# Loading tile 0 of the expert layers without the plan, and adding layer 1's residual behind the product

## The chip, the core and the metric

The kernel runs on one core of one Trainium2 chip. The metric is the device time of one execution in microseconds (us). The programs use five instruction streams: TensorE (PE in the profile, with its weight loads as PEld), VectorE (DVE), ScalarE (ACT), GpSimd (POOL) and SyncE (SP), which here only issues DMAs and reads values into registers. Everything is computed in float32.

## The reference

The input x is 4 batches of 512 tokens of width 256. Four blocks are added to it in turn: an attention with an MLP, a first mixture of experts, a second attention, a second mixture of experts. The change touches the two mixtures. Cut to what they compute:

```python
# layer 0: h = layernorm(x) @ W_in + b_in; 8 experts, two chosen per token
topv, topi = jax.lax.top_k(softmax(t @ W_gate + b_gate), 2)      # topv normalized to sum 1
mid  = relu(einsum('nd,edh->neh', t, W1) + b1)                   # 256 -> 1024
eout = einsum('neh,ehd->ned', mid, W2) + b2                      # 1024 -> 256
out  = einsum('ne,ned->nd', route, eout) @ W_out + b_out
...
# layer 1: 8 experts, one chosen per token
scores, idx = max(gates, axis=1), argmax(gates, axis=1)
h = gelu(x @ W1[idx] + b1[idx])                                  # 256 -> 512
o = (h @ W2[idx] + b2[idx]) * scores                             # 512 -> 256
x = x + o
```

## The kernel before

**Sorting tokens by expert.** Each token is computed only by the experts that it chose. `Dispatch.send` (L299) works out, for a group of tokens, the place of each in a DRAM buffer `sent`, in which expert e owns the rows from e * 2048 on. It counts the earlier tokens of each expert in `seen` by two small matmuls (`rank`, L311 and L312), adds the start of the expert's region (L317), picks the chosen expert's place (L318 to L321), casts it to an integer `slot` (L322), and scatters the rows by indirect DMAs from GpSimd (L325). A row has 258 numbers: the 256 features, the token's share for that expert, and the index of the row that the result goes back to. Before that, `sent` was filled with rows that lead nowhere (`clear`).

**The plan.** `Dispatch.plan` (L339) makes a list of tiles of 256 rows from the counts: a matmul `pn` (L343), its copy `n` (L345), a comparison of n with `full` (L347: how many tiles each expert has), a running sum, and for each tile its expert and its first row (L357 to L373). The number of tiles and these two lists are read into registers (`values_load` L369, `value_load` L379 and L380).

**The tiles.** `Dispatch.tiles` (L375) runs 20 tiles in layer 0 and 11 in layer 1 (`run`, L448), and up to 23 and 15 under a condition on the count. `load(i)` (L378) issues the DMAs of a tile, all on SP's queue: `rows` from `sent` (L382, 258 KB), the expert's W1 and W2 (`load_w1` L116, `load_w2` L121; together 2 MB in layer 0, 1 MB in layer 1) and its biases b1 and b2 (L387, L388; b2 is spread over all 128 partitions, 128 KB). In layer 1 it also gathers the residual of each row, which lies in `kept` in DRAM, into `y` by two indirect DMAs from GpSimd (L396). `turn` (L410) transposes the rows on TensorE (L414) and copies them to `inT` on VectorE (L416). `hidden` (L465) multiplies by W1 (L472) and applies bias and function into `mid`: on ScalarE (L476), in layer 0 on VectorE (L474) for every second chunk. It has three PSUM buffers `pm`. `give` (L419) prepares y: share * b2 on ScalarE in layer 0 (L429), share * b2 + residual on VectorE in layer 1 (L427). `project` (L479) multiplies mid by W2 (L485), and `take` (L431) adds share * product to y on VectorE (L432) and scatters y by an indirect DMA from GpSimd (L435): in layer 0 to `came`, in layer 1 to the output.

**Order and buffers.** The loop of `run` is: hidden(i), load(i + 1), turn(i + 1), give(i). Weights, biases, inT and mid have two buffers each, rows has two in layer 0 and four in layer 1, y two in layer 0 and four in layer 1. The weights' pool `wpool` also holds, by the same two tags, keys and values of the first stage, and between the layers what comes back from `came` (`bring`, L884, whose loads go by L888). Where no order is written out by hand, a scheduler places each engine's instructions by estimated times; an engine, and SP's queue, then runs them strictly in that order. The first stage is written out by hand for all engines except SP, the attention of layer 1 (from L1058 on) for TensorE only. So where SP's loads land in its queue is the scheduler's choice, except for those marked `keep_in_program_order`.

Of the kernel before, what the change touches and what calls it, by code (L numbers as in the profile page):

```python
# [25 lines left out]
NE = 8  # L26
# [17 lines left out]
def xattn_ffn_kernel(ctx: ExitStack, tc: tile.TileContext, a: dict, out: bass.AP):  # L44
# [69 lines left out]
    def load_w1(ap, n):  # L114
        w = wpool.tile([P, NC, n], F32, tag="w1", name="w1")
        nc.sync.dma_start(w, ap.rearrange("(c p) n -> p c n", p=P))  # L116
        return w
# [48 lines left out]
    def constants():  # L166
        nc.gpsimd.memset(nowhere[:, 0:TO], 0.0)
        nc.gpsimd.iota(
            nowhere[:, TO:ROW].bitcast(I32), pattern=[[0, 1]], base=NOWHERE, channel_multiplier=0
        )  # L170
        nc.gpsimd.memset(before, 1.0)
        nc.gpsimd.affine_select(
            before, before, pattern=[[1, P]], compare_op=ALU.is_gt, fill=0.0, base=0, channel_multiplier=-1
        )
        nc.gpsimd.memset(ones, 1.0)
        for e in range(NE):
            nc.gpsimd.memset(falling[:, :, e : e + 1], float(NE - e))
            nc.gpsimd.memset(region[:, :, e : e + 1], float(e * CAP))
        for j in range(CAP // TT):
            nc.gpsimd.memset(full[:, :, j : j + 1], float(j * TT))  # L180
        for i in range(TILES0):
            nc.gpsimd.memset(number[:, i, :], float(i))

# [96 lines left out]
    class Dispatch:  # L280
# [18 lines left out]
        def send(self, b, tts, chosen, psum, tag):  # L299

            pool, seen = self.pool, self.seen
            n, picks = chosen.shape[1:3]
            these = slice(tts[0], tts[-1] + 1)
            both = chosen[:, :, 0, :]
            if picks == 2:
                both = small.tile([P, n, NE], F32, tag="both", name="both")
                nc.vector.tensor_tensor(both, chosen[:, :, 0, :], chosen[:, :, 1, :], ALU.add)
            for t in tts:
                nc.vector.tensor_tensor(seen[:, t + 1, :], seen[:, t, :], both[:, t - tts[0], :], ALU.add)
            rank = psum.tile([P, n, NE], F32, tag=tag, name="rank")  # L310
            nc.tensor.matmul(rank, before, both, start=True, stop=False)  # L311
            nc.tensor.matmul(rank, ones, seen[:, these, :], start=False, stop=True)  # L312
            place = small.tile([P, n, NE], F32, tag="place", name="place")
            mine = small.tile([P, n, picks, NE], F32, tag="mine", name="mine")
            at = small.tile([P, n, picks], F32, tag="at", name="at")
            slot = pool.tile([P, n, picks], I32, tag="slot", name="slot", bufs=2)
            nc.vector.tensor_tensor(place, rank, region[:, 0:n, :], ALU.add)  # L317
            nc.vector.tensor_tensor(  # L318
                mine, chosen, place.unsqueeze(2).to_broadcast([P, n, picks, NE]), ALU.mult
            )  # L320
            nc.vector.tensor_reduce(at, mine, AX.X, ALU.add)  # L321
            nc.vector.tensor_copy(slot, at)  # L322
            for t in tts:
                for k, r in enumerate(self.rows):
                    i = nc.gpsimd.indirect_dma_start(  # L325
                        out=sent[self.layer][:, :],
                        out_offset=bass.IndirectOffsetOnAxis(ap=slot[:, t - tts[0], k : k + 1], axis=0),
                        in_=r[:, t, :],
                        in_offset=None,
                    )  # L330

                    tc.declare_no_dep(i.ins, group=self.group, reason="rows of their own")
                    tc.add_to_no_dep_group(self.group, i.ins)
            if tts[-1] == NT - 1:
                nxt = pool.tile([P, NT + 1, NE], F32, tag=f"seen{(b + 1) % 2}", name=f"seen{b + 1}")
                nc.vector.tensor_copy(nxt[:, 0, :], seen[:, NT, :])
                self.seen = nxt

        def plan(self, psum, tag):  # L339

# [1 line left out]
            pn = psum.tile([P, NE], F32, tag=tag, name="pn")  # L342
            nc.tensor.matmul(pn, ones, self.seen[:, 0, :], start=True, stop=True)  # L343
            n = small.tile([P, NE], F32, tag="n", name="n")
            nc.vector.tensor_copy(n, pn)  # L345
            more = small.tile([P, NE, CAP // TT], F32, tag="more", name="more")
            nc.vector.tensor_tensor(more, over(n, CAP // TT), full, ALU.is_gt)  # L347
            count = small.tile([P, NE], F32, tag="count", name="count")
# [23 lines left out]
            nc.vector.tensor_copy(self.row, first)  # L372
            nc.vector.tensor_copy(self.expert, e)  # L373

        def tiles(self, n_tiles, usual, n, w1_all, w2_all, b1_all, b2_all, func, tp, midp, pm_pool, po_pool, also):  # L375


            def load(i):  # L378
                e = nc.sync.value_load(self.expert[0:1, i : i + 1], min_val=0, max_val=NE - 1)  # L379
                row = nc.sync.value_load(self.row[0:1, i : i + 1], min_val=0, max_val=NE * CAP)  # L380
                rows = tp.tile([P, TT // P, ROW], F32, tag="rows", name="rows", bufs=2 + 2 * self.layer)
                nc.sync.dma_start(rows, sent[self.layer][bass.ds(row, TT), :].rearrange("(s p) w -> p s w", p=P))  # L382
                b1 = tp.tile([P, n // P], F32, tag="b1", name="b1")
                b2 = tp.tile([P, D], F32, tag="b2", name="b2")

                def biases():
                    nc.sync.dma_start(b1, b1_all[:, bass.ds(e * (n // P), n // P)])  # L387
                    nc.sync.dma_start(b2, b2_all[bass.ds(e, 1), :].to_broadcast([P, D]))  # L388

                y = None  # L390
                if self.layer == 1:
                    biases()
                    y = tp.tile([P, TT // P, D], F32, tag="y", name="y", bufs=4)
                    for u in range(TT // P):

                        nc.gpsimd.indirect_dma_start(  # L396
                            out=y[:, u, :],
                            out_offset=None,
                            in_=kept[:, :],
                            in_offset=bass.IndirectOffsetOnAxis(ap=rows[:, u, TO:ROW].bitcast(I32), axis=0),  # L400
                            bounds_check=N - 1,
                            oob_is_err=False,
                        )
                w1 = load_w1(w1_all[bass.ds(e, 1)].rearrange("o d n -> (o d) n"), n)
                w2 = load_w2(w2_all[bass.ds(e, 1)].rearrange("o k d -> (o k) d"), n)
                if self.layer == 0:
                    biases()
                return rows, w1, w2, b1, (b2, y)

            def turn(rows):  # L410
                ps = psT.tile([P, NC, TT // P, P], F32, tag="psT", name="psIn")
# [5 lines left out]
                return inT  # L417

            def give(rows, w2, added, mid):  # L419
                b2, y = added  # L420
                here = y is not None
                if not here:
                    y = tp.tile([P, TT // P, D], F32, tag="y", name="y")
                for u in range(TT // P):
                    share = rows[:, u, D:TO]
                    if here:
                        nc.vector.scalar_tensor_tensor(y[:, u, :], b2, share, y[:, u, :], ALU.mult, ALU.add)  # L427
                    else:
                        nc.scalar.mul(y[:, u, :], b2, share)  # L429

                def take(u, po):  # L431
                    nc.vector.scalar_tensor_tensor(  # L432
                        y[:, u, :], po, rows[:, u, D:TO], y[:, u, :], ALU.mult, ALU.add
                    )
                    i = nc.gpsimd.indirect_dma_start(  # L435
                        out=came[self.layer][:, :],
                        out_offset=bass.IndirectOffsetOnAxis(ap=rows[:, u, TO:ROW].bitcast(I32), axis=0),
                        in_=y[:, u, :],
                        in_offset=None,
                        bounds_check=came[self.layer].shape[0] - 1,  # L440
                        oob_is_err=False,
                    )
                    tc.declare_no_dep(i.ins, group=f"take{self.layer}", reason="rows of their own")
                    tc.add_to_no_dep_group(f"take{self.layer}", i.ins)

                project(mid, w2, po_pool, take)
# [66 lines left out]
    with tc.tile_pool(name="l0a", bufs=2) as lp, tc.tile_pool(name="l0tmp", bufs=2) as tp, tc.tile_pool(  # L513
# [274 lines left out]
        for b in range(B):  # L788
# [11 lines left out]
                *(memory[2:3] if b == 2 else ()), *((gates[3], chain(pad(8), memory[3])) if b == 3 else ()),  # L800
            )

    layer0.close()


# [40 lines left out]
    with tc.tile_pool(name="f0tmp", bufs=2) as tp, tc.tile_pool(  # L846
# [4 lines left out]
        send.plan(po_pool, "po")  # L851
        early = chain(places(heads), fetch(0))
        send.tiles(
            TILES0, 2 * N // TT + 4, HD, a["L0_ffn_W1"], a["L0_ffn_W2"], a["b1_0_col"], a["L0_ffn_b2"], AF.Relu,
            tp, midp, pm_pool, po_pool, early,
        )

# [6 lines left out]
    with tc.tile_pool(name="l1a", bufs=2) as lp, tc.tile_pool(name="l1s", bufs=1) as sp, tc.tile_pool(  # L864
# [193 lines left out]
        with tc.manual_schedule(engines={mybir.EngineType.PE}):  # L1058
# [12 lines left out]
            for i in range(-AHEAD, groups + 1):  # L1071
                if i + AHEAD in (NG, 2 * NG):
                    side.append(prepares[(i + AHEAD) // NG + 1])
                for n in range(2 * NT):
# [18 lines left out]
                            side += [finish(i // NG - 1), choose(i // NG - 1)]  # L1093
                    else:
                        step()
            while side:
                step()


    with tc.tile_pool(name="f1tmp", bufs=2) as tp, tc.tile_pool(  # L1100
# [3 lines left out]
    ) as pm_pool, tc.tile_pool(name="f1p_o", bufs=3, space=bass.MemoryType.PSUM) as po_pool:  # L1104
        send.plan(psT, "psT")
        send.tiles(
            TILES1, N // TT + 3, H1, a["L1_ffn_W1"], a["L1_ffn_W2"], a["b1_1_col"], a["L1_ffn_b2"], AF.Gelu,
            tp, midp, pm_pool, po_pool, iter(()),
        )

# [55 lines left out]
```

## Time and profile before

| | |
|---|---|
| runs of before (3) | 1078.2, 1081.53, 1085.03 us; median 1081.53 |
| the profiled execution | 1082.0 us |
| its span in the profile | 1080.3 us |
| PE busy | 981.3 us, 91% of the span |
| DVE, ACT, POOL busy | 519.2, 360.6, 295.5 us |
| layer 0's tiles, first product to last | 316.65 to 603.87 us |
| layer 1's tiles, first product to last | 978.22 to 1073.2 us |
| rows<-sent, landing | 2.8 us (median of 31) |
| weights, layer 0 / layer 1, landing | 7.1 / 6.1 us (medians of 40 and 22) |
| b2, landing | 6.7 us (median of 31) |
| gather of the residual / scatter to the output, landing | 5.2 / 4.1 us (medians of 22 and 22) |

The profile is of one execution. The page gives busy times of each engine, the chain of work that ended last and the costliest groups of instructions by source line. A line of the timeline has the start in us, the duration, the engine, the source line, the operation with output and inputs, the shape, the number of instructions run together, and in brackets the idle time of the engine before it and what ended it. "SPq" lines are SP issuing a DMA; the data lands later, and landing times run from the issue. "issue" means that nothing which the profile shows was waited for.

### The profile page before, as it was taken

Reading aid. Unit: us, or ns where it says so; the run is one execution under the profiler, and the core shown is the slowest. Engines: PE = TensorE matmul, PEld = TensorE weight load, DVE = VectorE, ACT = ScalarE, POOL = GpSimd, SP = SyncE. Lnnn points to the kernel's source line nnn. Section 1 sums busy time; section 2 is a strip of 40 time slices with the busy share of each in tenths; the row PEclk is TensorE's granted clock in tenths of the full one; section 3 lists DMA queues with packets and bytes.
Section 4 is the critical chain, followed back from the end, with each engine's and each line's share of the span. In section 5 each row is a group of like instructions: output and inputs, shape, how many; then the busy total and the mean of one; then the engine's idle time right before and its main releaser. Section 6 shows DMA issues by size and latency. Waiting matters only on the chain.

```text
span 1080.3 us, 14074 instructions
## 1 busy us (share of the span) xinstructions
PE 981.3 (91%) x4843; PEld 653.4 (60%) x4843; DVE 519.2 (48%) x1329; ACT 360.6 (33%) x628; POOL 295.5 (27%) x333
## 2 busy tenths in 40 slices
PE   5889999999759999999999689999999999948986
PEld 3556667575548888888888544333434334336775
DVE  5775675554642222222222168667767767132222
ACT  4444242324211111222211023555555565602221
POOL 3330242333332222111111273003623102113443
PEclk9989999999979999999999889999999999867999
DMA  6679999931164566656555402001101000017773
GB/s 203 222 183 249 247 248 242 247 104 39 40 211 145 192 204 202 202 188 206 180 187 187 165 21 58 11 6 56 39 12 58 20 2 20 20 48 228 218 202 94
DMA packets 113708, 146.00 MB, mean 135 GB/s; under 512 B 15060, under 2 KB 95197, under 8 KB 113632
## 3 DMA queue, kind: packets, MB, share of 16 engines
q1 hardware_dynamic: 107296, 130.29, 42.5%
q0 software_dynamic: 6336, 14.75, 4.1%
q8 instruction: 41, 0.67, 0.3%
q14 instruction: 35, 0.29, 0.1%
HBM read 86.71 MB, written 58.80 MB: 135 GB/s over the span
## 4 chain that ended last, share of the span: by engine, by line
PE 48%; issue 25%; POOL 9%; DMA 8%; DVE 7%; SPq 1%; ACT 1%; POOLq 0%; DVEq 0%
PE sc L958 12%; PE av L978 6%; PE pm L598 5%; PE po L604 4%; POOL came L435 3%; PE scT L958 3%; PE pm_sid L556 2%; PE pf L564 2%; DMA came<-y,rows 1%; PE pq L919 1%; PE psTr L877 1%; PE pd L579 1%; DMA rows<-sent 1%; DMA sent<-rows,slot 1%; PE po L1011 1%
## 5 line engine op out<-in xcount | busy, mean ns | idle before, releaser
L472 PE MATMUL pm<-inT,w 128*128 128x256 f32 x816 | 188.7, 390 | 14.2 <-DVE inT L416 8.3
L965 DVE TENSOR_REDUCE nm<-sc 128x1 f32<-128x512 f32 x256 | 164.2, 683 | 62.4 <-PE scT L958 60.0
L472 PEld LDWEIGHTS pm<-inT,w 128*128 128x128 f32 x816 | 158.4, 195 | 40.4 <-DVE inT L416 11.3
L485 PE MATMUL po<-w,mid 128*128 128x256 f32 x816 | 181.3, 379 | 0.0
L962 ACT ACTIVATE ex<-scT 128x512 f32<-128x512 f32 x256 | 138.6, 597 | 100.0 <-PE scT L958 99.2
L485 PEld LDWEIGHTS po<-w,mid 128*128 128x128 f32 x816 | 152.8, 190 | 19.6
L958 PE MATMUL sc<-kT,qT 32*128 32x512 f32 x512 | 161.6, 636 | 0.1
L958 PE MATMUL scT<-qT,kT 32*128 32x512 f32 x512 | 161.7, 649 | 0.0
L476 ACT ACTIVATE mid<-pm,b 128x256 f32<-128x256 f32 x124 | 58.7, 474 | 179.8 <-PE pm L472 146.8
L435 POOL DMA_INDIRECT came<-y,rows x40 | 39.3, 982 | 240.2 <-DVE y L432 240.2
L958 PEld LDWEIGHTS sc<-kT,qT 32*128 32x128 f32 x512 | 52.7, 183 | 61.2 <-DVE nm L965 46.5
L432 DVE SCALAR_TENSOR_TENSOR y<-po,rows,y 128x256 f32<-128x256 f32 x62 | 29.7, 481 | 123.8 <-PE po L485 120.8
L474 DVE TENSOR_SCALAR mid<-pm,b 128x256 f32<-128x256 f32 x80 | 38.7, 483 | 102.4 <-PE pm L472 102.4
L240 POOL TENSOR_TENSOR rstd<-var,halved 128x4 f32<-128x4 f32 (+1 forms) x32 | 27.9, 876 | 211.0 <-DVE var L239 188.9
L325 POOL DMA_INDIRECT sent<-rows,slot x48 | 48.0, 1000 | 90.4 <-DVE slot L322 43.0
L978 PE MATMUL av<-ex,va 128*32 128x512 f32 x512 | 70.7, 618 | 0.0
L598 PE MATMUL pm<-hT,w 128*128 128x512 f32 x128 | 63.8, 627 | 2.4 <-DVE hT L511 2.4
L604 PE MATMUL po<-w,mid 128*128 128x256 f32 x256 | 60.8, 383 | 0.0
L429 ACT ACTIVATE y<-b,rows 128x256 f32<-128x256 f32 x40 | 18.1, 500 | 127.5 <-DMA b<-in_L_ffn_b 108.1
L958 PEld LDWEIGHTS scT<-qT,kT 32*128 32x128 f32 x512 | 52.5, 186 | 12.8 <-issue 11.2
L604 PEld LDWEIGHTS po<-w,mid 128*128 128x128 f32 x256 | 48.1, 192 | 10.3 <-issue 4.5
L978 PEld LDWEIGHTS av<-ex,va 128*32 128x32 f32 x512 | 10.6, 109 | 50.6 <-issue 40.4
(236 smaller groups left out, 1182.5 us busy)
## 6 DMA issues: line engine op xcount, KB each, us to landing
w<-in_L_ffn_W SPq DMA_DIRECT2D x40, 1024.0 KB, 7.1
sent<-nowhere SPq DMA_DIRECT2D x32, 1161.0 KB, 19.8
w<-in_L_ffn_W SPq DMA_DIRECT2D x22, 512.0 KB, 6.1
rows<-sent SPq DMA_DIRECT2D x31, 258.0 KB, 2.8
y<-came SPq DMA_DIRECT2D x8, 512.0 KB, 7.9
b<-in_L_ffn_b SPq DMA_DIRECT2D x31, 128.0 KB, 6.7
x<-in_x SPq DMA_DIRECT2D x4, 512.0 KB, 5.4
c<-in_ctx SPq DMA_DIRECT2D x4, 512.0 KB, 7.1
```

What stands on the lines that cost most here:

```text
L325: i = nc.gpsimd.indirect_dma_start(out=sent[self.layer][:, :], out_offset=bass.IndirectOffsetOnAxis(ap=slot[:, t - tts[0], k : k + 1], axi ...
L435: i = nc.gpsimd.indirect_dma_start(out=came[self.layer][:, :], out_offset=bass.IndirectOffsetOnAxis(ap=rows[:, u, TO:ROW].bitcast(I32), ax ...
L472: nc.tensor.matmul(pm, w1[:, c, ts(k, P)], inT[:, c, :], start=c == 0, stop=c == NC - 1)
L474: nc.vector.tensor_scalar(mid[:, k, :], pm, bias[:, k : k + 1], 0.0, ALU.add, ALU.max)
L476: nc.scalar.activation(mid[:, k, :], pm, func, bias=bias[:, k : k + 1])
L485: nc.tensor.matmul(po, mid[:, k, ts(t, P)], w2[:, k, :], start=k == 0, stop=k == n - 1)
L598: nc.tensor.matmul(pm, w1_mlp[:, c, ts(k, P)], hT[:, c, :], start=c == 0, stop=c == NC - 1)
L604: nc.tensor.matmul(po, mid[:, k, ts(t, P)], w2_mlp[:, k, :], start=k == 0, stop=k == HD // P - 1)
L958: nc.tensor.matmul(sc, stay, move, start=True, stop=True)
L962: nc.scalar.activation(ex, sc, AF.Exp, scale=1.0 / DH**0.5)
L965: nc.vector.tensor_reduce(nm[:, t, head, 0:1], sc, AX.X, ALU.max, negate=True)
L978: nc.tensor.matmul(av[32 * head : 32 * head + 32, :], vas[b % 2][:, t, 4 * g + head, :], exs.pop((t, head)), start=t == 0, stop=t == NT - 1,)
```

## The change

- Tile 0 of a layer is now always of expert 0 and begins at row 0: `full` gets -1 for expert 0's first tile, so that this tile exists even with no token. Its addresses are constants.
- `ahead` issues tile 0's W1 and W2. It is called at the end of the first stage for layer 0, and in front of the last steps of the attention for layer 1. Tile 0's biases are issued before its rows.
- In `send`, the counts for the next batch are copied before the rank matmuls instead of behind the scatters; in `plan`, the copy of the counts is kept in program order.
- In layer 1 the residual is gathered into buffers `x` of its own (three), y has three buffers instead of four and is prepared by ScalarE in both layers, and `take` adds the residual on VectorE after the product.

The diff:

```diff
--- before.py
+++ after.py
@@ -178,6 +178,8 @@
             nc.gpsimd.memset(region[:, :, e : e + 1], float(e * CAP))
         for j in range(CAP // TT):
             nc.gpsimd.memset(full[:, :, j : j + 1], float(j * TT))
+
+        nc.gpsimd.memset(full[:, 0, 0:1], -1.0)
         for i in range(TILES0):
             nc.gpsimd.memset(number[:, i, :], float(i))
 
@@ -307,6 +309,10 @@
                 nc.vector.tensor_tensor(both, chosen[:, :, 0, :], chosen[:, :, 1, :], ALU.add)
             for t in tts:
                 nc.vector.tensor_tensor(seen[:, t + 1, :], seen[:, t, :], both[:, t - tts[0], :], ALU.add)
+            if tts[-1] == NT - 1:
+                nxt = pool.tile([P, NT + 1, NE], F32, tag=f"seen{(b + 1) % 2}", name=f"seen{b + 1}")
+                nc.vector.tensor_copy(nxt[:, 0, :], seen[:, NT, :])
+                self.seen = nxt
             rank = psum.tile([P, n, NE], F32, tag=tag, name="rank")
             nc.tensor.matmul(rank, before, both, start=True, stop=False)
             nc.tensor.matmul(rank, ones, seen[:, these, :], start=False, stop=True)
@@ -331,10 +337,6 @@
 
                     tc.declare_no_dep(i.ins, group=self.group, reason="rows of their own")
                     tc.add_to_no_dep_group(self.group, i.ins)
-            if tts[-1] == NT - 1:
-                nxt = pool.tile([P, NT + 1, NE], F32, tag=f"seen{(b + 1) % 2}", name=f"seen{b + 1}")
-                nc.vector.tensor_copy(nxt[:, 0, :], seen[:, NT, :])
-                self.seen = nxt
 
         def plan(self, psum, tag):
 
@@ -342,7 +344,8 @@
             pn = psum.tile([P, NE], F32, tag=tag, name="pn")
             nc.tensor.matmul(pn, ones, self.seen[:, 0, :], start=True, stop=True)
             n = small.tile([P, NE], F32, tag="n", name="n")
-            nc.vector.tensor_copy(n, pn)
+
+            tc.keep_in_program_order(nc.vector.tensor_copy(n, pn))
             more = small.tile([P, NE, CAP // TT], F32, tag="more", name="more")
             nc.vector.tensor_tensor(more, over(n, CAP // TT), full, ALU.is_gt)
             count = small.tile([P, NE], F32, tag="count", name="count")
@@ -372,40 +375,60 @@
             nc.vector.tensor_copy(self.row, first)
             nc.vector.tensor_copy(self.expert, e)
 
-        def tiles(self, n_tiles, usual, n, w1_all, w2_all, b1_all, b2_all, func, tp, midp, pm_pool, po_pool, also):
-
+        def ahead(self, n, w1_all, w2_all):
+
+
+            def weights(its):
+                return (
+                    load_w1(w1_all[its].rearrange("o d n -> (o d) n"), n),
+                    load_w2(w2_all[its].rearrange("o k d -> (o k) d"), n),
+                )
+
+            self.first, self.weights = weights(slice(0, 1)), weights
+
+        def tiles(self, n_tiles, usual, n, b1_all, b2_all, func, tp, midp, pm_pool, po_pool, also):
+
+            weights = self.weights
 
             def load(i):
-                e = nc.sync.value_load(self.expert[0:1, i : i + 1], min_val=0, max_val=NE - 1)
-                row = nc.sync.value_load(self.row[0:1, i : i + 1], min_val=0, max_val=NE * CAP)
-                rows = tp.tile([P, TT // P, ROW], F32, tag="rows", name="rows", bufs=2 + 2 * self.layer)
-                nc.sync.dma_start(rows, sent[self.layer][bass.ds(row, TT), :].rearrange("(s p) w -> p s w", p=P))
+                if i:
+                    e = nc.sync.value_load(self.expert[0:1, i : i + 1], min_val=0, max_val=NE - 1)
+                    row = nc.sync.value_load(self.row[0:1, i : i + 1], min_val=0, max_val=NE * CAP)
+                    its, at, to, b1s = bass.ds(e, 1), bass.ds(e, 1), bass.ds(row, TT), bass.ds(e * (n // P), n // P)
+                else:
+                    its, at, to, b1s = slice(0, 1), slice(0, 1), slice(0, TT), slice(0, n // P)
+                direct = self.layer == 1
+                rows = tp.tile([P, TT // P, ROW], F32, tag="rows", name="rows", bufs=4 if direct else 2)
                 b1 = tp.tile([P, n // P], F32, tag="b1", name="b1")
                 b2 = tp.tile([P, D], F32, tag="b2", name="b2")
+                w = []
 
                 def biases():
-                    nc.sync.dma_start(b1, b1_all[:, bass.ds(e * (n // P), n // P)])
-                    nc.sync.dma_start(b2, b2_all[bass.ds(e, 1), :].to_broadcast([P, D]))
-
-                y = None
-                if self.layer == 1:
+                    nc.sync.dma_start(b1, b1_all[:, b1s])
+                    nc.sync.dma_start(b2, b2_all[at, :].to_broadcast([P, D]))
+
+                if not i:
                     biases()
-                    y = tp.tile([P, TT // P, D], F32, tag="y", name="y", bufs=4)
+                nc.sync.dma_start(rows, sent[self.layer][to, :].rearrange("(s p) w -> p s w", p=P))
+                if direct and i:
+                    biases()
+                w = self.first if not i else weights(its)
+                if not direct and i:
+                    biases()
+                x = None
+                if direct:
+                    x = tp.tile([P, TT // P, D], F32, tag="x", name="xr", bufs=3)
                     for u in range(TT // P):
 
                         nc.gpsimd.indirect_dma_start(
-                            out=y[:, u, :],
+                            out=x[:, u, :],
                             out_offset=None,
                             in_=kept[:, :],
                             in_offset=bass.IndirectOffsetOnAxis(ap=rows[:, u, TO:ROW].bitcast(I32), axis=0),
                             bounds_check=N - 1,
                             oob_is_err=False,
                         )
-                w1 = load_w1(w1_all[bass.ds(e, 1)].rearrange("o d n -> (o d) n"), n)
-                w2 = load_w2(w2_all[bass.ds(e, 1)].rearrange("o k d -> (o k) d"), n)
-                if self.layer == 0:
-                    biases()
-                return rows, w1, w2, b1, (b2, y)
+                return rows, *w, b1, (b2, x)
 
             def turn(rows):
                 ps = psT.tile([P, NC, TT // P, P], F32, tag="psT", name="psIn")
@@ -417,21 +440,17 @@
                 return inT
 
             def give(rows, w2, added, mid):
-                b2, y = added
-                here = y is not None
-                if not here:
-                    y = tp.tile([P, TT // P, D], F32, tag="y", name="y")
+                b2, x = added
+                y = tp.tile([P, TT // P, D], F32, tag="y", name="y", bufs=2 if x is None else 3)
                 for u in range(TT // P):
-                    share = rows[:, u, D:TO]
-                    if here:
-                        nc.vector.scalar_tensor_tensor(y[:, u, :], b2, share, y[:, u, :], ALU.mult, ALU.add)
-                    else:
-                        nc.scalar.mul(y[:, u, :], b2, share)
+                    nc.scalar.mul(y[:, u, :], b2, rows[:, u, D:TO])
 
                 def take(u, po):
                     nc.vector.scalar_tensor_tensor(
                         y[:, u, :], po, rows[:, u, D:TO], y[:, u, :], ALU.mult, ALU.add
                     )
+                    if x is not None:
+                        nc.vector.tensor_tensor(y[:, u, :], y[:, u, :], x[:, u, :], ALU.add)
                     i = nc.gpsimd.indirect_dma_start(
                         out=came[self.layer][:, :],
                         out_offset=bass.IndirectOffsetOnAxis(ap=rows[:, u, TO:ROW].bitcast(I32), axis=0),
@@ -800,6 +819,8 @@
                 *(memory[2:3] if b == 2 else ()), *((gates[3], chain(pad(8), memory[3])) if b == 3 else ()),
             )
 
+        send.ahead(HD, a["L0_ffn_W1"], a["L0_ffn_W2"])
+
     layer0.close()
 
 
@@ -851,7 +872,7 @@
         send.plan(po_pool, "po")
         early = chain(places(heads), fetch(0))
         send.tiles(
-            TILES0, 2 * N // TT + 4, HD, a["L0_ffn_W1"], a["L0_ffn_W2"], a["b1_0_col"], a["L0_ffn_b2"], AF.Relu,
+            TILES0, 2 * N // TT + 4, HD, a["b1_0_col"], a["L0_ffn_b2"], AF.Relu,
             tp, midp, pm_pool, po_pool, early,
         )
 
@@ -1093,6 +1114,7 @@
                             side += [finish(i // NG - 1), choose(i // NG - 1)]
                     else:
                         step()
+            send.ahead(H1, a["L1_ffn_W1"], a["L1_ffn_W2"])
             while side:
                 step()
 
@@ -1104,7 +1126,7 @@
     ) as pm_pool, tc.tile_pool(name="f1p_o", bufs=3, space=bass.MemoryType.PSUM) as po_pool:
         send.plan(psT, "psT")
         send.tiles(
-            TILES1, N // TT + 3, H1, a["L1_ffn_W1"], a["L1_ffn_W2"], a["b1_1_col"], a["L1_ffn_b2"], AF.Gelu,
+            TILES1, N // TT + 3, H1, a["b1_1_col"], a["L1_ffn_b2"], AF.Gelu,
             tp, midp, pm_pool, po_pool, iter(()),
         )
```

## The prediction

> **What bounds the kernel now.** I read the page first: matmuls are busy for 91% of the span, so time can come only from stretches where TensorE waits. Near the change these are the start of each layer's expert tiles and the eleven tiles of layer 1. The waits from 960 us to the end (who, for what: total us, times, longest):
>
> ```profile
> DVE y L427 <- DMA y<-kept,rows: 55.8, 12, 8.0
> PE pm L472 <- DVE inT L416: 8.3, 7, 2.6
> ```
>
> VectorE stands at L427 until the gathered residual has landed. The windows of layer 1, cut at tile starts (stretch, length, then busy us of PE, PEld, DVE, ACT, POOL; granted clock, DMA share, GB/s):
>
> ```profile
> 1004.90:1012.35 7.45, 7.45 (x36) 6.36 (x37) 2.33 (x6) 1.90 (x4) 3.71 (x4) 1.00 0.73 217
> 1028.60:1038.80 10.20, 7.60 (x36) 6.38 (x36) 2.25 (x6) 1.90 (x4) 4.08 (x5) 0.97 0.73 195
> 1056.90:1066.00 9.10, 7.59 (x37) 6.36 (x37) 2.24 (x6) 1.90 (x4) 4.06 (x5) 1.00 0.55 164
> ```
>
> A tile holds about 7.4 us of TensorE and takes up to 10.2. The timeline of one shows why: the copy that TensorE needs for the next tile is queued behind L427.
>
> ```profile
> 1054.93 0.88 DVE L427 SCALAR_TENSOR_TENSOR y<-b,rows,y 128x256 f32<-128x256 f32 x2 [7.05 <-DMA out_x<-y,rows]
> ...
> 1056.12 0.68 DVE L416 COPY inT<-psIn 128x512 f32<-128x512 f32 x1
> ...
> 1056.86 3.72 PE L472 MATMUL pm<-inT,w 128*128 128x256 f32 x16 [1.70 <-DVE inT L416]
> ```
>
> The two starts, layer 0 and layer 1 (rows issued, weights issued, first product):
>
> ```profile
> 310.83 0.41 SPq L382 DMA_DIRECT2D rows<-sent  x1
> 311.51 0.38 SPq L116 DMA_DIRECT2D w<-in_L_ffn_W  x1
> 316.65 9.51 PE L472 MATMUL pm<-inT,w 128*128 128x256 f32 x32 [1.85 <-DMA w<-in_L_ffn_W]
> ```
>
> ```profile
> 967.54 0.96 POOL L325 DMA_INDIRECT sent<-rows,slot  x1 [0.30 <-issue]
> 970.22 0.41 SPq L382 DMA_DIRECT2D rows<-sent  x1
> 978.22 5.46 PE L472 MATMUL pm<-inT,w 128*128 128x256 f32 x12 [4.12 <-DMA w<-in_L_ffn_W]
> 980.33 1.28 ACT L476 ACT_TABLE_LOAD   x1 [20.63 <-PE pm L472]
> ```
>
> Both rows loads wait for the last scatter to land (967.54 to 970.22: 2.7 us), not for the plan; the weights, issued behind them, land last. Finally the landing of b2, asked of line 388 in layer 1, on which the forecast turns:
>
> ```profile
> DMA to landing us min/median/max: 3.7/5.2/5.6
> ```
>
> **What the Trainium skill says.** "DMA: Bandwidth & Descriptors", section "Issuing engines are not separate DMA queues": DMAs from every engine run on the same 16 DMA engines and interleave, so b2 waits behind weights, rows and gathers. The 3.7 against 5.6 us agrees. "ScalarE: Activation LUTs", "What ACT_TABLE_LOAD costs": about 1283 ns; the 1.28 us at 980.33 agrees. Its "Table sets" section has copy and identity in every set, so scaling b2 between two Gelus should load nothing; no trace here shows that pair. "TensorE: Matmul & The Clock Gate", "What's actually happening": the clock starts throttled and needs activity. The stretch 970 to 978 has clock 0.50, and that stays so.
>
> **Layer 0, tile 0.** W1, W2 and biases (4 issues) leave the SP queue behind the plan and go where layer 0's last batch is stored. SP is idle there except for two stores; DMA share is 0.31 from 298 to 312, which hides them; uncovered, a weight load takes 7.1 us by the page. Rows(0) cannot go earlier: the last scatter (308.10) lands at 310.8. The order of the built changed kernel (the built order, below) puts one transpose of tile 1 ahead of tile 0's product, so TensorE next waits for rows(1). From 313.32 + 0.36 to 315.06 two plan values cost 1.4 us, so rows(1) issues at 310.83 + 0.41 + 1.4 = 312.6, lands 2.8 later at 315.4; product at 315.75 instead of 316.65. **Gain 0.9** (0 if rows(1) is late, at most 1.1, the product then following inT at 315.5). The other 19 tiles keep their 14.26 us pitch, all TensorE.
>
> **Layer 1, tile 0.** W2 and W1 are put between the loads of came and the stores into qT. They wait for the combines of batches 0 and 1 (last transpose 622.2); qT is issued at 636.7 and 5 to 6 us of landing lie between, so cost 0; if that cover were gone, qT would move by that landing. The pinned plan copy lets slot follow place directly: 962.2 instead of 962.9, scatter at about 962.5 instead of 963.66, so rows(0) at 969.0 (970.2 if GpSimd gains nothing). Rows(1) 1.8 later, 970.8, lands 973.5; its transposes precede tile 0's product: 974.7 instead of 978.22. But ScalarE now scales b2 for tiles 0 **and 1** before the table load: b2(1) issues at 972.0, lands at 976.0, two scalings (0.45 each, L429's rows) to 976.95, table 978.25. Tile 0's last hidden activation then ends at about 980.5 instead of 985.3: **gain 4.8** (4.1 to 5.3).
>
> **Layer 1, steady state.** L427 leaves VectorE (2 x 0.48 per tile); two adds come (128x256 f32, 0.42 each by L609's record). Gathers get three buffers of their own and run one tile further ahead; a gather (3.0 to 6.6 us to land) then has over 15 us. So inT no longer waits and TensorE's own 7.4 is the floor. The wait goes elsewhere. In ScalarE's built order y(k+1) stands before the four activations of tile k. It needs b2(k+1), whose issue follows b1(k+1), which waits until mid(k-1) is done, its buffer's last reader. Call that end T:
>
> - b1 issues at once (mid ended 985.30, b1 985.33), b2 0.6 later, lands after L;
> - two scalings, 0.9, and 0.1 of signals;
> - four activations: three products wait in PSUM; the fourth needs a freed buffer: 0.47 + 0.2 + 1.06 (product start to activation, 988.31 to 989.37) + 0.47 = 2.2.
>
> The pitch is p = L + 3.8, floored at 7.4. Queued behind y on ScalarE is mid, and for mid waits TensorE's second product. L is 3.7 (tiles at 985 and 993, rows issued 2.8 us or more earlier) to 5.6 (rows issued 1.4 us before b2, held back by the scatters). With the scatters no longer behind gather waits, rows should go earlier, about 4 us before T; but more MB per us cross the engines (some 1.9 MB a tile: 240 GB/s at p = 8, where 231 took share 0.81). I take L = 4.2, p = 8.0.
>
> Sum: from tile 0's last activation to tile 9's is 985.30 to 1061.09 = 75.8 now, 9p after. Tile 9 to 10 is 9.1 now and 7.5 after (nothing ahead of mid(10)): 1.6. The last add costs 0.4 before the last scatter. Layer 1 gains 4.8 + 75.8 - 9p + 1.6 - 0.4 = 81.8 - 9p: 9.8 at p = 8.0, shown as 10. With layer 0's 0.9: 11. The profiled execution took 1082.0 (span 1080.3 and 1.7 around it), so 1071.0; it stands 0.5 above the median 1081.53, so **1070.5**.
>
> The memset of full and the earlier copy of seen are small work on idle engines: 0 (0.2 each uncovered).
>
> **Rivals.**
> 1. TensorE becomes the bound: b2 lands in 3.7 or less. p = 7.4 to 7.5, gain 14.3 to 15.2 plus 0.9: 1065.4 to 1066.3. For it: the uncrowded landings; against: 1.9 MB in 7.4 us is more than any window of this stage moved.
> 2. The gain goes into the new wait: b2 lands at its present median, 5.2; p = 9.0, layer 1 gains 0.8: 1079.8. For it: later tiles all showed 5.1 to 5.6.
> 3. Slower: the same loop with crowded landings. From L = 5.4 it costs more than the start gains. Layer 0's b2, behind 1 MB weight loads, lands in 6.7 by the page's median: p = 10.5, layer 1 loses 12.7: 1093.3. Against it: in layer 1 no landing above 5.6 was seen, and the weights here are half.
> 4. The change doesn't act on the start: rows(1) or b2(1) hold it as the weights did; 4 us less gain, 1074.5.
>
> **Chances.** Forecast (1067 to 1075, with 4 at its edge) 0.52, rival 1 0.20, rival 2 0.21, rival 3 0.07. The likeliest case's own range is 1067 to 1075. The range reaches over rivals 1 and 2: 1065 to 1081. One per cent, about what a measurement of this kernel can tell from no change, is 10.8 us, so faster means below 1070.7: all of rival 1 and half of the forecast, 0.46; slower by that much only rival 3's far half, 0.04; the rest 0.50.
>
> **What would show it.** After: no wait of VectorE on the gather; TensorE's wait on inT gone; instead ScalarE waits at the scaling of y (L446 of the changed kernel) for b2 in layer 1, then TensorE waits for mid. Pitch minus b2's landing near 3.8. First products near 315.7 and 974.7. Wrong if ScalarE does not wait for b2 (rival 1), if the first gathers still hold VectorE, or if qT starts later against the end of layer 0.

## The result and the profile after

The changed kernel took 1070.6 us (median of 8 runs, 1067.61 to 1074.36), the kernel before 1080.7 us beside it (8 runs, 1073.97 to 1085.03). The ratio is 0.9917, 95% interval 0.9892 to 0.9942. The forecast was 1070.5. It started from a median of 1081.5 and gained 11.0; measured side by side the gain is 10.1. The profiled execution took 1067.61 us, with a span of 1065.8.

Where before VectorE stood at the scaling until the gather had landed, the waits of the changed kernel from 945 us to the end show another place (who, for what: total us, times, longest):

```profile
POOL xr L423 <- DMA rows<-sent: 33.4, 9, 6.3
...
ACT y L446 <- DMA b<-in_L_ffn_b: 28.6, 6, 5.7
...
ACT y L446 <- DVE y L453: 13.5, 3, 4.6
...
PEld pm L491 <- ACT mid L495: 7.8, 8, 3.0
...
ACT y L446 <- DMA out_x<-y,rows: 6.4, 1, 6.4
...
PE pm L491 <- ACT mid L495: 5.1, 4, 2.6
```

No line has VectorE waiting for the gather, and none has a product of TensorE waiting for inT. ScalarE now waits at the scaling of y, and TensorE for the hidden activations. The three waits put down to L453 begin the scaling 3.9 to 4.0 us after b2's issue, as the waits named b2 do; so b2 is the likelier releaser there. SP's own waits show why b2 is asked for so late:

```profile
SPq L407 <- ACT mid L495: 22.3, 9, 4.7
```

The load of b1, in front of b2 on the queue, stands nine times until the activations that read the old b1 are done. The timeline of one tile shows the whole loop:

```profile
1015.65 0.35 SPq L407 DMA_DIRECT2D b<-in_b_col  x1
...
1016.19 0.34 SPq L408 DMA_DIRECT2D b<-in_L_ffn_b  x1
...
1020.72 0.91 ACT L446 ACTIVATE y<-b,rows 128x256 f32<-128x256 f32 x2 [5.09 <-DMA b<-in_L_ffn_b]
...
1021.53 1.18 ACT L495 ACTIVATE mid<-pm,b 128x256 f32<-128x256 f32 x3
...
1022.03 1.13 PE L491 MATMUL pm<-inT,w 128*128 128x256 f32 x4 [0.44 <-ACT mid L495]
1023.20 0.47 ACT L495 ACTIVATE mid<-pm,b 128x256 f32<-128x256 f32 x1 [0.50 <-PE pm L491]
...
1023.70 0.34 SPq L407 DMA_DIRECT2D b<-in_b_col  x1
...
1024.24 0.35 SPq L408 DMA_DIRECT2D b<-in_L_ffn_b  x1
```

Activations end at 1015.62, b1 goes at 1015.65, b2 at 1016.19; 4.5 us later the scalings start, then the activations, the last of which waits for a product that needed a freed PSUM buffer; they end at 1023.67, and b1 goes at 1023.70. The pitch, from one tile's last activation to the next tile's, is 8.05 here. Three such windows (columns as in the prediction):

```profile
1000.64:1007.99 7.35, 7.35 (x38) 6.47 (x37) 2.51 (x6) 2.58 (x7) 4.33 (x5) 1.00 0.78 234
1015.62:1023.67 8.05, 7.61 (x38) 6.38 (x37) 2.51 (x6) 2.46 (x7) 2.39 (x3) 1.00 0.88 261
1023.67:1033.02 9.35, 7.62 (x38) 6.39 (x37) 2.51 (x6) 2.47 (x7) 6.13 (x6) 1.00 0.75 241
```

In the first, TensorE is busy throughout; in the second it loses 0.4 us, in the third 1.7. The two starts, layer 0 and then layer 1 in two pieces:

```profile
308.98 2.16 SPq L412 DMA_DIRECT2D rows<-sent  x2
...
313.57 0.47 PE L437 MATMUL psIn<-ident,rows 128*128 128x128 f32 x1 [0.59 <-DMA rows<-sent]
...
313.84 6.48 PE L491 MATMUL pm<-inT,w 128*128 128x256 f32 x22
```

```profile
964.31 2.36 SPq L412 DMA_DIRECT2D rows<-sent  x2
966.86 0.36 SPq L407 DMA_DIRECT2D b<-in_b_col  x1
967.40 0.35 SPq L408 DMA_DIRECT2D b<-in_L_ffn_b  x1
967.93 0.38 SPq L116 DMA_DIRECT2D w<-in_L_ffn_W  x1
```

```profile
970.23 3.77 PE L491 MATMUL pm<-inT,w 128*128 128x256 f32 x12
...
973.81 0.91 ACT L446 ACTIVATE y<-b,rows 128x256 f32<-128x256 f32 x2 [5.70 <-DMA b<-in_L_ffn_b]
...
974.73 1.28 ACT L495 ACT_TABLE_LOAD   x1
```

In layer 1 TensorE begins early, at 970.23, but ScalarE's scaling for tile 1 waits until 973.81 for a b2 issued at 967.40, with the table load and tile 0's activations behind it.

The spans of the two profiles differ by 14.5 us. I cut both into five stretches: to the issue of layer 0's rows(0); on to layer 0's first product; on to the issue of qT; on to SP's last store into `kept`; on to the end. Before: 310.83, 5.82, 320.05, 313.05, 130.55 us; after: 308.98, 4.86, 318.67, 312.24, 121.05. So 9.50 us come from layer 1's tiles, 0.96 from layer 0's start, and 4.04 from stretches for which the forecast had nothing. Those vary from profile to profile: rows(0) was issued at 308.98 to 315.05 in the thirteen profiles of this study, and qT to `kept`, which no edit touches, took 309.84 to 317.65. The latter goes with the clock granted to TensorE in it: 309.84 to 310.53 us at a mean of 0.994 to 0.995, 312.20 to 312.32 at 0.989, 313.05 and 313.08 at 0.984, 314.67 at 0.978, 317.65 at 0.968. All experiments are therefore read from `kept` onward, beside the timed ratios.

### The profile page after: what moved, and what is told of

It is laid out like the page before. It is cut to its first block, busy times and chain, and to the rows that moved or that the text cites. A ratio compares the mean times of both kernels' runs of the same rounds, so it can differ in the third digit from the quotient of the medians.

```text
span 1065.8 us, 14095 instructions
## 1 busy us (share of the span) xinstructions
PE 974.6 (91%) x4843; PEld 650.0 (61%) x4843; DVE 522.3 (49%) x1329; ACT 367.0 (34%) x650; POOL 295.1 (28%) x334
## 5 line engine op out<-in xcount | busy, mean ns | idle before, releaser
L491 PE MATMUL pm<-inT,w 128*128 128x256 f32 x816 | 185.5, 384 | 5.1 <-ACT mid L495 5.1
L491 PEld LDWEIGHTS pm<-inT,w 128*128 128x128 f32 x816 | 156.2, 192 | 29.2 <-ACT mid L495 7.8
L446 ACT ACTIVATE y<-b,rows 128x256 f32<-128x256 f32 x62 | 28.1, 500 | 197.1 <-DMA b<-in_L_ffn_b 132.3
L495 ACT ACTIVATE mid<-pm,b 128x256 f32<-128x256 f32 x124 | 56.5, 470 | 112.5 <-PE pm L491 92.5
L623 PEld LDWEIGHTS po<-w,mid 128*128 128x128 f32 x256 | 47.8, 190 | 10.3 <-issue 4.5
L439 DVE COPY inT<-psIn 128x512 f32<-128x512 f32 x31 | 21.4, 691 | 43.0 <-PE psIn L437 43.0
```

What stands on the lines that cost most here:

```text
L491: nc.tensor.matmul(pm, w1[:, c, ts(k, P)], inT[:, c, :], start=c == 0, stop=c == NC - 1)
L495: nc.scalar.activation(mid[:, k, :], pm, func, bias=bias[:, k : k + 1])
L623: nc.tensor.matmul(po, mid[:, k, ts(t, P)], w2_mlp[:, k, :], start=k == 0, stop=k == HD // P - 1)
```

## The experiments

Parts are in us, from the profile of each kernel: `kept` stored to tile 0's last activation, from there to tile 9's (nine pitches), tile 9 to 10, tile 10 to the end of the span, and their sum.

| kernel | to tile 0 | tiles 0 to 9 | 9 to 10 | to the end | sum |
|---|---|---|---|---|---|
| before | 35.55 | 75.79 | 9.13 | 10.08 | 130.55 |
| changed | 33.45 | 69.62 | 7.34 | 10.64 | 121.05 |
| residual alone | 36.02 | 69.21 | 7.35 | 10.61 | 123.19 |
| tile 0 alone | 30.77 | 75.75 | 11.77 | 10.13 | 128.42 |
| scaling in program order | 31.14 | 65.68 | 7.34 | 10.66 | 114.82 |
| four buffers for b1, b2 | 33.01 | 66.27 | 7.34 | 10.63 | 117.25 |
| order and buffers | 30.73 | 65.66 | 7.35 | 10.61 | 114.35 |
| second load of b2 | 34.25 | 92.86 | 7.34 | 10.66 | 145.11 |
| plain load beside b2 | 32.89 | 73.59 | 7.34 | 10.66 | 124.48 |
| four buffers for y | 32.74 | 70.76 | 7.34 | 10.61 | 121.45 |
| weights held, first form | 32.91 | 71.92 | 7.35 | 10.61 | 122.79 |
| weights held | 31.45 | 70.62 | 7.34 | 10.66 | 120.07 |
| biases before rows | 33.31 | 69.24 | 7.34 | 10.59 | 120.48 |

Each row is one profile. The tiles of six of these kernels have the same loop (changed, residual alone, four buffers for y, both with weights held, biases before rows); the mean of their nine pitches goes from 7.69 to 7.99. A difference of 0.3 in one profile's mean pitch is thus within their spread.

**The two halves.** The first kernel has only the residual's part of the diff on top of the kernel before; the second is the changed kernel with the residual put back in front of the product (shown from the changed kernel, its core):

```diff
-                    nc.scalar.mul(y[:, u, :], b2, rows[:, u, D:TO])
+                    nc.vector.scalar_tensor_tensor(y[:, u, :], b2, share, y[:, u, :], ALU.mult, ALU.add)
...
-                        nc.vector.tensor_tensor(y[:, u, :], y[:, u, :], x[:, u, :], ALU.add)
```

> The kernel before with one part of the change alone: layer 1's residual gathered into its own tile and added behind the product; tile 0 still waits for the plan. Theory (the pitch of layer 1 is set by the loop mid(k-1), b1, b2, y(k+1), mid(k)): pitch from tile 0's last activation to tile 9's about 7.7 us as in the changed kernel instead of 8.4, so 6 to 7 us from there and 1 us net from tile 10 and the tail: about 1073 us against 1080.7. The stretch from the residual's store to tile 0's last activation stays at 35.6 us. Rival (the gain comes from tile 0's start or from what lies upstream): within 2 us of the kernel before.

> The changed kernel with its residual put back in front of the product: only tile 0's loads ahead of the plan are left, with the pinned copy and the earlier copy of seen. Theory: 0.9 us in layer 0, 2 to 4 us in layer 1's start (scatter 0.9 earlier, the product 3 us earlier), the pitch of layer 1 stays at about 8.4 us: about 1077 us. Rival (the start carries most of the gain): 1072 to 1073.

Residual alone: 1075.14 us, ratio 0.9927 (0.9906 to 0.9949). Its mean pitch is 7.69, close to the changed kernel's 7.74; 7.36 us are gained from `kept` on, all of it behind tile 0. Tile 0 alone: 1074.66 us, ratio 0.9946 (0.9923 to 0.9970). The mean pitch stays at 8.42, with the old wait:

```profile
DVE y L450 <- DMA y<-kept,rows: 55.8, 13, 7.8
```

Tile 0 comes 4.78 us earlier (2 to 4 were expected), but tile 10 gives 2.64 back (11.77 against 9.13, behind late gathers), so 2.1 remain, and 0.90 in layer 0. By the parts the rival falls: from `kept` on the residual gains 7.36 us, tile 0 alone 2.1. By the times it does not: the intervals of the two ratios overlap, and 1074.66 lies between the 1077 of the theory and the rival's 1072 to 1073. The timed gain of tile 0 alone, 3.2 to 8.3 us, is more than the 3.0 that these parts explain. Its profile is short between qT and `kept` (309.84), but the clock granted there was also higher, 0.994 against 0.984 in the kernel before, and in all thirteen profiles the length of this stretch goes with that clock; the edit is not needed to explain it. Where the rest of the timed gain comes from stays open.

**ScalarE's order.**

```diff
-                    nc.scalar.mul(y[:, u, :], b2, rows[:, u, D:TO])
+                    m = nc.scalar.mul(y[:, u, :], b2, rows[:, u, D:TO])
+                    if x is not None:
+                        tc.keep_in_program_order(m)
```

> The changed kernel with layer 1's scaling of b2 held in program order, so that y(k) stands behind the activations of tile k on ScalarE and no activation stands behind a scaling that waits for the next tile's b2. Theory: tile 0's last activation comes 2 to 3 us earlier and the pitch falls from 7.74 to TensorE's own 7.4, nine times 0.34 is 3: about 1065.5 against 1070.6. Rival (TensorE, y's buffers or the DMA engines set the pitch): pitch stays at 7.7, at most the start's 2 us are gained: 1068.5 to 1070.6.

1063.75 us, ratio 0.9843 (0.9793 to 0.9893), where the changed kernel's interval was 0.9892 to 0.9942. Tile 0 comes 2.3 us earlier, and every later pitch is 7.34 or 7.35 but the first, 6.91. The timeline of one tile:

```profile
1026.61 0.47 ACT L497 ACTIVATE mid<-pm,b 128x256 f32<-128x256 f32 x1 [0.34 <-PE pm L493]
1027.47 0.47 ACT L497 ACTIVATE mid<-pm,b 128x256 f32<-128x256 f32 x1 [0.39 <-PE pm L493]
1028.34 0.47 ACT L497 ACTIVATE mid<-pm,b 128x256 f32<-128x256 f32 x1 [0.39 <-PE pm L493]
1028.71 0.90 ACT L446 ACTIVATE y<-b,rows 128x256 f32<-128x256 f32 x2
```

The scaling has no bracket: it waits for nothing. The activations wait only for TensorE's products. The window of this tile is filled by TensorE while the DMA engines move 244 GB/s:

```profile
1021.46:1028.81 7.35, 7.35 (x38) 6.47 (x37) 2.58 (x6) 2.69 (x8) 5.76 (x6) 1.00 0.77 244
```

So neither TensorE nor the DMA engines set the pitch of 7.74. The order of one engine's queue did, by putting the activations behind whatever the next tile's scaling waits for: b2, or a buffer of y.

**The other end of the loop.** Buffers instead of order, so that b1 and b2 are issued before the activations of the tile before last are done:

```diff
-                b1 = tp.tile([P, n // P], F32, tag="b1", name="b1")
-                b2 = tp.tile([P, D], F32, tag="b2", name="b2")
+                b1 = tp.tile([P, n // P], F32, tag="b1", name="b1", bufs=4 if direct else 2)
+                b2 = tp.tile([P, D], F32, tag="b2", name="b2", bufs=4 if direct else 2)
```

> The changed kernel with four buffers instead of two for b1 and b2 in layer 1, ScalarE's order unchanged: b1 and b2 of a tile no longer wait until the activations of the tile two before are done. Theory: b2 lands before its scaling, the pitch falls to 7.4, the start stays (b2 of tile 1 still lands at the same place): 3 us less, about 1067.5. Rival: pitch 7.7, 1070.6.

1066.94 us, ratio 0.9864 (0.9815 to 0.9913). This interval overlaps that of the changed kernel, so the evidence is in the parts: seven of the nine pitches are 7.34 or 7.35, the mean 7.36, below the 7.69 to 7.99 of the uncut loop; tile 0 stays (33.01). Cutting the loop at either end removes it. Both cuts, with y's four buffers:

> The changed kernel with scaling in program order, four buffers for b1 and b2, and four for y in layer 1. Theory: TensorE's own 7.35 us already sets every tile with the order alone, so nothing is left for the buffers: within 1 us of that kernel, about 1063.5. Rival (early landings of b2 help besides the order): 1061 or less.

1064.01 us, ratio 0.9869 (0.9818 to 0.9920): nothing beyond the order alone, as expected.

**Lengthening the loop.**

```diff
                     nc.sync.dma_start(b1, b1_all[:, b1s])
+                    if direct and i:
+                        b3 = tp.tile([P, D], F32, tag="b3", name="b3")
+                        nc.sync.dma_start(b3, b2_all[at, :].to_broadcast([P, D]))
                     nc.sync.dma_start(b2, b2_all[at, :].to_broadcast([P, D]))
```

> The changed kernel with a second, unused load of b2 (128 KB) between b1 and b2 in layer 1, for every tile but the first; it adds work, the result is the same. Theory (pitch = landing of b2 + 3.6 after the end of the activations two tiles back): the issue costs 0.57 us more and the bytes 0.6 at some 220 GB/s, so the pitch goes from 7.7 to 8.3 to 8.9 and the stretch from the residual's store to the end grows by 6 to 10 us: about 1078 against 1070.6. Rival (another wait sets the pitch, b2 has slack): pitch stays at 7.7, within 2 us of the changed kernel.

1092.24 us, ratio 1.0104 (1.0049 to 1.0158): slower than before. The direction is the theory's, the size is not: the pitch went to 10.32, not to 8.3 to 8.9. From tile 2 on, the scaling starts 5.6 to 6.3 us after b2's issue (982.87 to 988.93 for tile 2), where the changed kernel took 3.7 to 4.5 for all of these tiles but one. One more broadcast, a load that spreads one row over all partitions, costs about 2 us of landing, not 0.6. The same 128 KB from 128 rows of W2 instead of 128 times one row:

```diff
-                        nc.sync.dma_start(b3, b2_all[at, :].to_broadcast([P, D]))
+                        nc.sync.dma_start(b3, self.w2_all[its, 0:P, :].rearrange("o k d -> (o k) d"))
```

> The changed kernel with the extra 128 KB load between b1 and b2 read from 128 different rows of 1 KB of the expert's second weight matrix, not 128 times from the one row of b2; every tile but the first of layer 1; it adds work, the result is the same. If the bytes and packets cost the 2.1 us by which a second broadcast delayed b2: pitch 10.3 again, landing of b2 6.0. If it is the broadcast from one row that is slow: landing 4.2 to 4.8, pitch 8.3 to 8.9.

The mean pitch is 8.18 (8.3 to 8.9 was expected) and the scalings start 3.5 to 4.9 us after b2's issue from tile 2 on. The landing of the plain load (L410), then of b2 (L411), in that one kernel:

```profile
DMA to landing us min/median/max: 2.0/2.4/3.2
```

```profile
DMA to landing us min/median/max: 3.7/4.2/5.1
```

So the same bytes in the same place delay b2 little when they are not a broadcast. The pitch is 0.44 above the changed kernel's; the extra issue takes 0.53 us on SP's queue, but 0.44 is not far above the spread of the profiles.

**The long pitch.** One pitch of the changed kernel was 9.35, with the wait for `out_x` above. y has three buffers, so the scaling of tile 8 needs the one that tile 5's scatters read. Their adds were done by 1020.06, but they stood in GpSimd's queue behind gathers that waited for rows:

```profile
1019.50 1.05 POOL L423 DMA_INDIRECT xr<-kept,rows  x1 [3.56 <-DMA rows<-sent]
...
1025.31 1.00 POOL L454 DMA_INDIRECT out_x<-y,rows  x1 [0.30 <-DMA rows<-sent]
...
1030.07 0.91 ACT L446 ACTIVATE y<-b,rows 128x256 f32<-128x256 f32 x2 [6.39 <-DMA out_x<-y,rows]
```

The second scatter landed 4.6 us after its issue, at 1029.9. The test gives y a fourth buffer:

```diff
-                y = tp.tile([P, TT // P, D], F32, tag="y", name="y", bufs=2 if x is None else 3)
+                y = tp.tile([P, TT // P, D], F32, tag="y", name="y", bufs=2 if x is None else 4)
```

> The changed kernel with four instead of three buffers for y in layer 1. Theory: the one long pitch, 9.35 us from tile 6 to tile 7, is a wait for a scatter that still reads y's buffer; it falls to about 8, the other pitches stay between 7.3 and 8.1. Rival (b2 is late there as well): it stays above 9.

The expectation failed: no scaling waits for `out_x` any more, but two pitches are long, 9.12 and 9.25, and there ScalarE waits for b2, 5.6 and 5.7 us after its issue. So there are two kinds of long pitch. The scatter makes one: with four buffers for b1 and b2 the longest pitch, 7.94, has a scaling that starts at 1035.08, just after a scatter landed (at 1034.9) and 6.9 us after b2's issue, and the 9.44 of the residual alone is put down to `out_x` too. The other is a late b2. What now and then adds 1.7 us to a landing of b2 stays open, and four buffers for y have no gain to show.

**Tile 1's b2.** In the changed kernel it took 6.4 us to the scaling. Which traffic held it?

```diff
+                if direct and i == 1:
+                    hold = tp.tile([1, 1], F32, tag="hold", name="hold")
+                    nc.sync.dma_start(hold, b2[0:1, 0:1])
-                w = self.first if not i else weights(its)
+                w = self.first if not i else weights(its, direct and i == 1)
```

> The changed kernel with one 4 byte transfer that reads b2 of layer 1's tile 1, put on SP's queue behind that load and ahead of tile 1's two weight loads, so that the weights do not enter the DMA engines before b2 has landed. Theory (b2 of tile 1 took 6.4 us because it shares the DMA engines with tile 1's 1 MB of weights): it lands in about 4 us and tile 0's last activation comes 1.5 to 2.5 us earlier, at about 31.5 after the residual's store instead of 33.45. Rival (rows and gathers ahead of it hold it): landing stays near 6 us, 33.4.

The edit shown is the second form; its last argument pins the place of W1's load. The first form lacks that argument and tells nothing: the scheduler had put the weight loads (967.08, 967.64) ahead of the held transfer (972.37). With the pin:

> The changed kernel with the 4 byte transfer that reads b2 of layer 1's tile 1 really ahead of tile 1's weight loads on SP's queue (in the run before, the weights had stayed in front of it). Theory A (tile 1's weights crowd b2): it lands in about 4 us instead of 5.7 to 6.4, tile 0's last activation at 31 to 31.5 after the residual's store instead of 32.7 to 33.5. Theory B (the rows of tile 1, issued 1.1 us ahead of it, hold it): landing 5.5 or more, activation 32.5 or more; the weights of tile 1 land later and may delay tile 1 by 2 to 4 us.

```profile
977.51 0.34 SPq L410 DMA_DIRECT2D b<-in_L_ffn_b  x1
981.11 0.72 SPq L419 DMA_DIRECT2D hold<-b  x1
982.04 0.41 SPq L116 DMA_DIRECT2D w<-in_L_ffn_W  x1
```

```profile
977.21 0.91 ACT L451 ACTIVATE y<-b,rows 128x256 f32<-128x256 f32 x2 [12.54 <-DMA rows<-sent]
981.18 0.91 ACT L451 ACTIVATE y<-b,rows 128x256 f32<-128x256 f32 x2 [3.06 <-DMA b<-in_L_ffn_b]
```

The scaling starts 3.67 us after b2's issue, though tile 1's rows are still issued 1.1 us ahead of it, and tile 0 comes at 31.45. In the four profiles that load tile 1 as the changed kernel does (changed, four buffers for b1 and b2, four for y, weights held in the first form) it starts 5.7 to 6.4 us after the issue. Both figures are as theory A, the weights, has them; theory B, that the rows hold b2, had 5.5 or more. It gains no time: with the weights late, the next pitch is 8.37. The counterpart:

```diff
+                if direct and i == 1:
+                    biases()
                 nc.sync.dma_start(rows, sent[self.layer][to, :].rearrange("(s p) w -> p s w", p=P))
-                if direct and i:
+                if direct and i > 1:
                     biases()
```

> The changed kernel with b1 and b2 of layer 1's tile 1 issued ahead of that tile's rows, not behind them. Theory B (the rows hold b2): b2 is issued 0.5 us earlier and lands in 4 to 4.5 us instead of 5.7 to 6.4; the scaling of tile 1 starts 2 us earlier. Theory A (the weights crowd it): landing 5.5 or more, and 0.5 us earlier at most. In both the rows of tile 1 go out 1.1 us later, which may delay the first product by as much.

The scaling of tile 1 started 4.83 us after b2's issue (972.19 to 977.02), but released by the rows, issued at 972.84. The wait had moved, and b2's own landing is hidden behind it: it took 4.83 us at most. That is less than the 5.5 or more of theory A, but in this kernel the weights also come later, 1.2 us behind b2 (973.41) and not 0.5. So weights right behind b2 are enough to hold it; that the rows have no part in it is not shown.

## Why the prediction was right, point by point

- **VectorE stands for the gather, inT behind it.** Right: both waits are gone, and the residual alone takes 6.6 us out of nine pitches, more than twice the spread among the profiles' nine pitches (2.7 us).
- **Layer 0, tile 0: 0.9.** Right: 0.96 by the profile, 0.90 in tile 0 alone, and TensorE does wait for rows(1) at 313.57.
- **Weights ahead cost nothing for qT.** Layer 0's first product to qT took 320.05 before and 318.67 after: no loss seen.
- **Layer 1, tile 0: 4.8.** Too much, and only because of the scaling of b2: tile 0 alone, where ScalarE has nothing ahead of the table load, gains 4.78. Rows(0) came 0.9 us earlier against `kept` (1.2 forecast), the first product 3.0 (3.5 forecast), tile 0's last activation only 2.1. The failed term is "b2(1) issues at 972.0, lands at 976.0": the 4.0 were 6.4, with tile 1's 1 MB of weights issued right behind, and 3.67 with the weights held. The Trainium skill's "DMA: Bandwidth & Descriptors", section "Issuing engines are not separate DMA queues", says that DMAs interleave on the same 16 engines, whichever engine started them. The section does not say what a later load on the same queue does to an earlier one; here the two figures show it. I had applied it to what is ahead of b2 and not to what follows. Rival 4 is thus half true.
- **Layer 1, pitch L + 3.8, L = 4.2.** The mechanism is shown by cutting the loop (order, buffers, both) and by lengthening it. In eight of the nine pitches L, from b2's issue to the scaling, was 3.7 to 4.5, p - L was 3.52 to 3.67, and the mean p was 7.53, not 8.0. The ninth, 9.35, was no landing of b2 but the wait for y's buffer. The forecast put nothing on y's three buffers, and its "scatters no longer behind gather waits" holds for VectorE's waits only: GpSimd stands 33.4 us, nine times, at gathers that wait for rows, with scatters behind them. With that pitch the mean is 7.74: nine times 0.26 is 2.4 us more gain. This and the start's 2.7 less cancel, so 9.5 stands beside the 9.8 forecast. That is luck: median and parts agree because errors cancel, not because each term was exact.
- **Tile 9 to 10, the last add.** 9.13 to 7.34 gains 1.8 (1.6 forecast); the tail lost 0.56 (0.4 forecast).
- **Clock at the start: stays at 0.50.** Right up to the first product (0.50 from 964.00 to 970.20). Behind it the clock rose sooner than before: the first twelve products took 3.77 us at a mean of 0.73, where before they took 5.46 at 0.51. ScalarE was not ready before 974.73, which hides it.
- **Scaling between two Gelus loads no table.** Layer 1's tiles have one ACT_TABLE_LOAD, at 974.73, though scalings and activations alternate; the Trainium skill's "ScalarE: Activation LUTs", section "Table sets", agrees.
- **Rivals.** Rival 1's argument against, that the DMA engines could not bring a tile in 7.4 us, was wrong: with the order pinned they moved 231 to 264 GB/s in the single tiles from 992.08 to 1043.50, each 7.34 or 7.35 us long, and 251 on average, which is 1.84 MB a tile. Rival 2's pitch, 9.0, appears only in single tiles. Rival 3 is a real mechanism, as the doubled load shows at p = 10.3 (10.7 us slower than before, by the medians), but the change itself does not come near it.
- **Memset and earlier copy of seen: 0.** Not tried alone, so not shown.

## What to carry to other kernels

A wait that is taken from one engine's queue can go to another engine's: here from VectorE's to ScalarE's. Write out who stands behind the new waiting instruction and close the loop (load, wait, reader, buffer free, load), since its length is the pitch where it exceeds the work of the busiest engine. Such a loop can be cut at either end, by order on the engine (here 6.2 us from `kept` on, by the parts) or by buffers (here 3.8); an instruction whose input is for the next tile should stand behind this tile's work. When a landing time is estimated, count also the large loads that are issued right after it.

## What was not expected of the hardware

Spreading one 1 KB row over 128 partitions is much slower than its 128 KB suggest: a second such load between b1 and b2 delayed b2 by about 2 us (to 5.6 to 6.3, from 3.7 to 4.5), and a plain 128 KB load in the same place hardly at all (3.5 to 4.9); in one kernel the plain load landed in 2.4 us and the spread one behind it in 4.2 (medians). Why is not shown. Where the weights were held, the trace has b2's 128 packets of 1 KB: they begin spread over 2.0 us, 978.76 to 980.73, and 123 of them take under 0.1 us each, so the time lies in when they begin and not in how long each takes.
